# Three of four batches written out by channels, in a convolution-attention kernel on one core

## The chip, the cores and the metric

The kernel runs on one core of one Trainium2 chip. A core has five engines, which run side by side and wait for one another by semaphores: TensorE (PE in the profile, PEld for its weight loads), VectorE (DVE), ScalarE (ACT), GpSimd (POOL) and SyncE (SP). In this kernel nearly all DMAs are issued by SP, one after another in the order of its queue. The metric is device time in microseconds, the median of several runs.

## The reference

The input `x` has 4 batches of 128 channels by 64 x 64 positions; the 4096 positions are the tokens. All is float32.

```
# layer 0, per batch
q, k, v = wq @ x, wk @ x, wv @ x                 # 64 channels each
x  = x + wo @ (softmax(k^T q, axis=2) v)         # 4096 x 4096 scores
# layer 1, on tokens t = x^T
t  = t + softmax(causal(LN(t) Wq (LN(t) Wk)^T / sqrt(128))) LN(t) Wv
w  = batchnorm(LN(t) W)                          # mean and variance over batches and tokens
y_0 = 0;  y_n = sigmoid(w_n + y_(n-1) V^T)       # a recurrence over the 4096 tokens
out = (t + y)^T
```

## The kernel before, in words

The function `fast_path` does all the work; a second, general path stands behind a branch on `flag` and is not entered here.

**Attention.** Batches go one after another, and in each batch layer 0 and then layer 1, in eight blocks of 512 tokens. A list `items` holds pairs of key tiles; a loop over it interleaves on TensorE the scores of one item with the values of the item two before. Everything else (projections, normalization, transposes) is cut into steps that generators hand out at due slots (`push`, `waiting`, `side`). The result of a block stays in the tile `xs`, by tokens. In `finish1`, the end of a block of layer 1, `third` replaces that block in `xs` by `w`, the input of the recurrence. The sum `t`, which the output still needs, is saved to DRAM before that, in one of two forms. For the batches below `BY_C`, the step `kept` transposes it in squares of 32 x 32 on VectorE and writes it by channels to `x2c` with four DMAs. For the others, one DMA stores it by tokens to `x2t` (in `first`).

**Start.** SP issues eight loads of `x` for batch 0 (L426), then the transfers `swap` of the keys (L541) and the loads of `x` by tokens (`tokens0`, L585), in an order that the scheduler chose.

**Recurrence.** It is computed for 256 chunks of 16 tokens at once (`STEPS` 16, `NCH` 256). Ten steps of a warm-up (`WARM`) give each chunk a start value, then 16 steps follow. In each step and for each of the four batches there is a product with V on TensorE (L1153), an add of `w` on VectorE (L1155, tile `z`) and a sigmoid on ScalarE (L1158). The last block's end in `third` is written out apart (`final`): two half projections (L825), two copies into `xs` (L827), and the function `warm`, which issues products that nobody reads. A test compares the last states with the start values (`gap`, `count`, `total`) and sets `flag`.

**Output.** For the batches by channels, `xc` is loaded from `x2c`, four loads for each batch (L1093). After every step, `add` sums state and `xc` for those batches on GpSimd (L1165, tile `sum`, three buffers) and one DMA writes the step out (L1167). The adds and these DMAs are kept in program order. For the batches by tokens, `xr` is loaded from `x2t` (L1103); `residual` transposes the states on TensorE (L1182), adds them to `xr` on VectorE (L1184) and writes pieces of 512 KB (L1187). The `residual` of the last batch stands at the program's end, behind the test.

```
for s in range(-WARM, STEPS):
    for b in range(B):
        step(b, s)
    if s >= 0:
        add(s)
```

Of the kernel before, what the change touches and what calls it, by code (L numbers as in the profile page):

```python
# [9 lines left out]
F32 = mybir.dt.float32  # L10
AF = mybir.ActivationFunctionType
ALU = mybir.AluOpType
AX = mybir.AxisListType
PSUM = bass.MemoryType.PSUM

P = 128
BLK = 512
# [1 line left out]
LN_EPS = 1e-5  # L19
BN_EPS = 1e-5  # L20
STEPS = 16
BY_C = 2


@with_exitstack
def general_path(
# [259 lines left out]
    with tc.tile_pool(name="wx", bufs=1) as wxp, tc.tile_pool(name="fwork", bufs=3) as wk:  # L286
# [28 lines left out]
        with tc.tile_pool(name="ys", bufs=3) as ysp, tc.tile_pool(  # L315
# [13 lines left out]
            for kb in range(nblk):  # L329
# [15 lines left out]
                K = STEPS // S  # L345
                for b in range(BY_C):
                    oc = ysp.tile([P, S, K], F32, tag="oc", name="oc")
                    nc.vector.tensor_copy(oc, o[:, b].rearrange("p (k s) -> p s k", s=S))
                    nc.sync.dma_start(out=out_c[b, :, :, ts(kb, K)], in_=oc)
                op = ps_o.tile([P, B - BY_C, P], F32, tag="o", name="oT_ps")  # L350
                for b in range(BY_C, B):
                    nc.tensor.transpose(op[:, b - BY_C, :], o[:, b, :], ident)
                oT = ysp.tile([P, B - BY_C, P], F32, tag="oT", name="oT")
                nc.vector.tensor_copy(oT, op)
# [5 lines left out]
def fast_path(  # L360
# [22 lines left out]
    nc = tc.nc  # L383
    B, C, N = x.shape
    M = c_wqT.shape[1]
    assert C == P and M == P // 2 and N % CHUNK == 0
    NT = N // P
    NB = N // BLK
    TPB = BLK // P
    SHIFT = 32.0  # L390
    LOW, HIGH = 1e-25, 1e25
    WARM, TOL = 10, 2e-6
# [12 lines left out]
    xs = xpool.tile([P, B, N], F32, name="xs")  # L405


    x2c = dram.tile([BY_C, NB, S, Q, BLK], F32, name="x2c")
    x2t = dram.tile([B - BY_C, N, P], F32, name="x2t")
# [18 lines left out]
    ident = const.tile([P, P], F32, name="ident")  # L428
    make_identity(nc, ident)
    ones = const.tile([P, 1], F32, name="ones")  # L430
# [30 lines left out]
    good = const.tile([P, 2], F32, name="good")  # L461
# [20 lines left out]
    with tc.tile_pool(name="batch", bufs=1) as batch, tc.tile_pool(name="rows", bufs=2) as rowp, tc.tile_pool(  # L482
        name="prob", bufs=4
    ) as prob, tc.tile_pool(name="work", bufs=2) as wk, tc.tile_pool(name="stat", bufs=4) as stat, tc.tile_pool(
        name="ps_s", bufs=2, space=PSUM
    ) as ps_s, tc.tile_pool(name="ps_a", bufs=1, space=PSUM) as ps_a, tc.tile_pool(
        name="ps_m", bufs=2, space=PSUM
    ) as ps_m:

        def misc(name):  # L490
            return ps_m.tile([P, BLK], F32, tag="m", name=name)
# [90 lines left out]

        def tokens0(b, g):

            nc.sync.dma_start(  # L585
                out=xs[:, b, ts(g, BLK)].rearrange("p (j c) -> p j c", c=P),
                in_=xT[b, ts(g, BLK)].rearrange("(j p) c -> p j c", p=P),
            )

        def rows1(b, g):  # L590
            ps = misc("r_ps")
            nc.tensor.matmul(ps, lhsT=g1, rhs=bs[b].xhT[:, ts(g, BLK)], start=True, stop=True)
            r = rowp.tile([P, BLK], F32, tag="r", name="rows1")
            nc.scalar.copy(r, ps)
            bs[b].next.append(r)
# [100 lines left out]
        def in_range(last):  # L696

            r = recs.rearrange("p l b t -> p (l b t)")
            r = r[:, -TPB:] if last else r[:, :-TPB]
            r2 = wk.tile([P, BLK], F32, tag="den", name="r2")[:, : r.shape[-1]]  # L700
            nc.vector.tensor_scalar(r2, r, LOW, None, ALU.is_ge)
            nc.vector.tensor_scalar(r, r, HIGH, None, ALU.is_le)
            nc.vector.tensor_tensor(r, r, r2, ALU.mult)
            nc.vector.tensor_reduce(good[:, 1:2] if last else good[:, 0:1], r, AX.X, ALU.add)
# [50 lines left out]
        def finish1(b, g):  # L755
            agg, den = bs[b].agg, bs[b].den
            mem = {}
            final = b == B - 1 and g == NB - 1

            def warm(n, rhs):  # L760

                ps = ps_s.tile([P, 2 * BLK], F32, tag="s", name="warm_ps")
                for _ in range(n):
                    tc.keep_in_program_order(
                        nc.tensor.matmul(ps[:, : BLK // 2], lhsT=ident, rhs=rhs, start=True, stop=True)
                    )
# [51 lines left out]
            def third():  # L818

                to = xs[:, b, ts(g, BLK)].rearrange("p (s c) -> p s c", s=STEPS)  # L820
                if final:
                    in_range(True)
                    for k in range(2):
                        wp = misc("wx_ps")[:, : BLK // 2]
                        nc.tensor.matmul(wp, lhsT=wfc, rhs=mem["xhT"][:, ts(k, BLK // 2)], start=True, stop=True)  # L825
                        nc.vector.bn_stats(ends[:, 3 + 6 * k : 9 + 6 * k], wp)
                        nc.scalar.copy(to[:, :, ts(k, CPB // 2)], wp.rearrange("p (c s) -> p s c", s=STEPS))  # L827
                    warm(6, xs[:, b, ds(g * BLK, BLK // 2)])
                    return
                wp = misc("wx_ps")  # L830
                nc.tensor.matmul(wp, lhsT=wf, rhs=mem["xhT"], start=True, stop=True)
                nc.vector.bn_stats(stats[:, b * NB + g], wp)  # L832
                if b == B - 1 and g == NB - 2:
                    ahead()
                    in_range(False)
                nc.scalar.copy(  # L836
                    to.rearrange("p s (j q u) -> p s j q u", q=Q, j=TPB),
                    wp.rearrange("p (q j u s) -> p s j q u", q=Q, j=TPB, s=STEPS),
                )
# [244 lines left out]
    with tc.tile_pool(name="xr", bufs=1) as xrp, tc.tile_pool(name="y", bufs=2) as yp, tc.tile_pool(  # L1084
        name="sums", bufs=3
    ) as sums, tc.tile_pool(
        name="ps_y", bufs=1, space=PSUM
    ) as ps_y, tc.tile_pool(name="ps_r", bufs=4, space=PSUM) as ps_r:

        xc = xrp.tile([P, BY_C, NCH, STEPS], F32, name="xc")  # L1090
        for b in range(BY_C):
            for c in range(Q):
                nc.sync.dma_start(  # L1093
                    out=xc[ts(c, S), b].rearrange("r (g k) s -> r g (k s)", g=NB),
                    in_=x2c[b, :, :, c].rearrange("g r n -> r g n"),
# [3 lines left out]
        by_chunk = lambda t: t.rearrange("b (h q s) c -> b h q s c", q=P, s=STEPS)  # L1099
        xr = xrp.tile([P, B - BY_C, HALVES, STEPS, P], F32, name="xr")  # L1100
# [19 lines left out]
        by_step = xs.rearrange("p b (g s c) -> p b s g c", s=STEPS, c=CPB)  # L1120
        start = xrp.tile([P, B, NCH + 1], F32, name="start")
        nc.gpsimd.memset(start[:, :, 0:1], 0.0)
        prev = [None] * B
        grid = lambda t: t.rearrange("p (g c) -> p g c", c=CPB)
        pair = lambda t: t.rearrange("p (h q) -> p h q", q=P)
# [8 lines left out]
        def states(b, s):  # L1134
            if b < BY_C:
                return by_step[:, b, s]
            return pair(early[:, b - BY_C, s]) if s < TPB else late[:, b, s // TPB - 1, s % TPB]
# [20 lines left out]
                nc.scalar.activation(y, shaped(z), AF.Sigmoid, bias=shift)  # L1158
            prev[b] = start[:, b, :NCH] if s == -1 else y

        def add(s):

            t = sums.tile([P, BY_C, NCH], F32, tag="sum", name="sum")
            by_grid = lambda t: t.rearrange("p b (g c) -> p b g c", c=CPB)
            ins = nc.gpsimd.tensor_tensor(by_grid(t), by_step[:, :BY_C, s], by_grid(xc[:, :, :, s]), ALU.add)  # L1165
            tc.keep_in_program_order(ins)
            tc.keep_in_program_order(nc.sync.dma_start(out=out_c[:, :, s].rearrange("b c k -> c b k"), in_=t))  # L1167

        for s in range(-WARM, STEPS):
            for b in range(B):  # L1170
                step(b, s)
            if s >= 0:
                add(s)

        def residual(b):

            for h in range(HALVES):
                for s0 in range(0, STEPS, TPB):
                    part = slice(s0 - TPB, s0 + TPB)
                    ps = ps_r.tile([P, TPB, P], F32, tag="r", name="yT_ps")  # L1180
                    for j in range(TPB):
                        nc.tensor.transpose(ps[:, j], states(b, s0 + j)[:, h], ident)  # L1182
                    t = xr[:, b - BY_C, h, ds(s0, TPB)]
                    nc.vector.tensor_tensor(t, t, ps, ALU.add)  # L1184
                    if s0 % (2 * TPB):
                        tc.keep_in_program_order(
                            nc.sync.dma_start(out=by_chunk(out_t)[b - BY_C, h, :, part], in_=xr[:, b - BY_C, h, part])  # L1187
                        )

        for b in range(BY_C, B - 1):  # L1190
            residual(b)


        gap = xrp.tile([P, B], F32, name="gap")
        for b in range(B):
            ps = ps_y.tile([P, NCH], F32, tag=f"y{b}", name="gap_ps")
            nc.tensor.matmul((grid if b < BY_C else pair)(ps), lhsT=ident, rhs=prev[b], start=True, stop=False)
            nc.tensor.matmul(ps, lhsT=minus, rhs=start[:, b, 1:], start=False, stop=True)
            sq = yp.tile([P, NCH], F32, tag=f"y{b}", name="sq")
            nc.scalar.activation(sq, ps, AF.Square, accum_out=gap[:, b : b + 1])  # L1200
        count = xrp.tile([P, B + 2], F32, name="count")
        nc.vector.tensor_scalar(count[:, :B], gap, TOL * TOL, None, ALU.is_le)
        nc.vector.tensor_copy(count[:, B:], good)
        total = xrp.tile([P, 1], F32, name="total")
        nc.vector.tensor_reduce(total, count, AX.X, ALU.add)
        tp = ps_y.tile([1, 1], F32, tag="y0", name="tp")
        nc.tensor.matmul(tp, lhsT=total, rhs=ones, start=True, stop=True)
        nc.vector.tensor_scalar(flag, tp, P * (B + 2 * B * NT) - 0.5, None, ALU.is_lt)
        residual(B - 1)


# [62 lines left out]
```

## Time and profile before

| | |
|---|---|
| runs | 2058.35, 2058.4 and 2059.66 us; median 2058.4 us |
| profiled execution | 2059.29 us, of which the profile's span is 2057.6 us |
| mean granted TensorE clock | 0.997 |
| busy over the span | TensorE 99%, VectorE 72%, ScalarE 48%, GpSimd 7% |
| attention | from the start to 1974.3 us, the copy of the last values |
| recurrence | the first product of a step at 1991.94, the last sigmoid until 2039.5 us |
| GpSimd's adds | 16 of 1.54 us, from 2010.9 us on |
| `xc` loads | 8 of 512 KB, issued from 1974.3 to 1981.4 us |
| `xr` loads | 4 of 1024 KB, issued from 1981.9 to 1988.7 us |

Times in the profile count from the start of the span. A timeline line gives the start, the length, the engine, the source line, the operation, output and inputs, and in brackets how long the engine had been idle before and what ended that. A line of a tile's view gives the shortest, median and longest duration in nanoseconds and the first and last start. A line of stretches gives the stretch, its length, the busy time of TensorE, its weight loads, VectorE, ScalarE and GpSimd with their counts, the granted clock, the share of the DMA engines and GB/s.

### The profile page before, as it was taken

The page shows a single profiled execution, that of the slowest core. Times are in us where ns is not written, and L with a number is a line of the kernel's source. Part 1 is how long each engine was busy: PE and PEld are TensorE (multiplying, and loading weights), DVE is VectorE, ACT ScalarE, POOL GpSimd, SP SyncE. Part 2 cuts the span into 40 slices and gives each one's busy share as a digit, 9 for nine tenths or more (in the row PEclk, how much of TensorE's full clock was granted, in tenths as well). Part 3 has the DMA queues.
Part 4 walks back from the last instruction along what each step waited for, and adds up shares of the span by engine and source line. Part 5 has one row for each costly group of instructions (what it writes and reads, how often), then busy time and mean ns, then how long its engine had stood idle before and what let it go on. Part 6 is the DMA issues. An engine that isn't in the chain of part 4 may idle for free. (4 is left out here: it accounts for less than half of the span.)

```text
span 2057.6 us, 30790 instructions
## 1 busy us (share of the span) xinstructions
PE 2039.1 (99%) x11646; PEld 909.0 (44%) x11646; DVE 1486.6 (72%) x2862; ACT 988.8 (48%) x1071; POOL 137.5 (7%) x237
## 2 busy tenths in 40 slices
PE   9999999999999999999999999999999999999998
PEld 3643355444333345444433335444433334544456
DVE  4899877554889987555689987654488998765568
ACT  5666633333666653333466663233366665333346
POOL 1000011000000011000000001100000000100004
PEclk9999999999999999999999999999999999999999
DMA  4111021231201112223111101123000111111064
GB/s 113 43 23 23 12 42 37 55 76 36 58 5 20 22 22 42 47 63 71 27 43 22 22 12 42 42 67 77 16 17 2 23 22 22 47 36 32 16 161 174
DMA packets 237293, 89.03 MB, mean 43 GB/s; under 512 B 174688, under 2 KB 219232, under 8 KB 236624
## 3 DMA queue, kind: packets, MB, share of 16 engines
q1 hardware_dynamic: 236128, 86.42, 17.7%
q8 instruction: 93, 1.52, 0.3%
q14 instruction: 64, 0.52, 0.1%
q0 software_dynamic: 288, 0.39, 0.1%
q10 hardware_dynamic: 720, 0.16, 0.0%
HBM read 45.84 MB, written 36.89 MB: 40 GB/s over the span
## 5 line engine op out<-in xcount | busy, mean ns | idle before, releaser
L931 DVE TENSOR_TENSOR dsum<-dsum,p 128x1024 f32<-128x1024 f32 x676 | 826.3, 1222 | 428.7 <-ACT p L907 308.1
L905 ACT ACTIVATE p<-s_ps,nshift 128x1024 f32<-128x1024 f32 x512 | 569.3, 1116 | 317.7 <-PE s_ps L891 311.4
L907 ACT ACTIVATE p<-s_ps 128x1024 f32<-128x1024 f32 (+2 forms) x288 | 274.2, 952 | 609.4 <-PE s_ps L900 607.1
L951 PE MATMUL acc<-p,v 64*64 64x512 f32 x4096 | 543.0, 590 | 0.0
L891 PE MATMUL s_ps<-swap,kr 64*64 64x512 f32 x2048 | 538.9, 591 | 1.4 <-ACT p L905 0.9
L891 PE MATMUL s_ps<-kr 64*64 64x512 f32 x2048 | 524.9, 591 | 0.0
L900 PE MATMUL s_ps<-rows,xhT 128*128 128x512 f32 (+3 forms) x1152 | 502.9, 559 | 0.0
L959 PE MATMUL acc<-p,xh 128*128 128x512 f32 (+3 forms) x1152 | 500.8, 557 | 0.0
L959 PEld LDWEIGHTS acc<-p,xh 128*128 128x128 f32 x1152 | 216.2, 190 | 244.3 <-issue 234.2
L900 PEld LDWEIGHTS s_ps<-rows,xhT 128*128 128x128 f32 x1152 | 214.0, 190 | 243.3 <-issue 203.2
L951 PEld LDWEIGHTS acc<-p,v 64*64 64x64 f32 x4096 | 166.6, 133 | 272.5 <-issue 251.6
L891 PEld LDWEIGHTS s_ps<-swap,kr 64*64 64x64 f32 x2048 | 151.4, 133 | 131.6 <-issue 107.8
L891 PEld LDWEIGHTS s_ps<-kr 64*64 64x64 f32 x2048 | 140.7, 133 | 138.0 <-issue 133.8
L663 POOL TENSOR_TENSOR ln_rstd<-ln_var,mhalf 128x4 f32<-128x4 f32 x64 | 68.1, 1065 | 1099.5 <-DVE ln_var L661 1099.5
L939 DVE TENSOR_TENSOR dsum<-dsum,p 128x256 f32<-128x256 f32 (+1 forms) x120 | 55.4, 498 | 64.6 <-POOL p L911 64.6
L649 DVE SCALAR_TENSOR_TENSOR xs<-o_ps,recs,xs 128x128 f32<-128x128 f32 x256 | 74.5, 341 | 3.1
L679 DVE TENSOR_SCALAR xh<-xs,ln_mv,ln_rstd 128x128 f32<-128x128 f32 x252 | 70.3, 343 | 2.2
L911 POOL TENSOR_SCALAR_AFFINE_SELECT p<-p 128x128 f32<-128x128 f32 x128 | 35.9, 304 | 486.2 <-ACT p L907 473.8
L658 DVE BATCH_NORM_STATS2 ln_st<-xs 128x6 f32<-128x128 f32 x256 | 63.3, 270 | 0.0
L929 DVE COPY dsum<-p 128x1024 f32<-128x1024 f32 x60 | 41.0, 683 | 15.4 <-ACT p L907 10.8
L1155 DVE SCALAR_TENSOR_TENSOR z<-xs,scale,y_ps 128x256 f32<-128x256 f32 x100 | 44.6, 481 | 9.1 <-PE y_ps L1153 7.7
L836 ACT COPY xs<-wx_ps 128x512 f32<-128x512 f32 x31 | 18.1, 585 | 65.6 <-DVE stats L832 61.5
(148 smaller groups left out, 993.7 us busy)
## 6 DMA issues: line engine op xcount, KB each, us to landing
xs<-in_xT SPq DMA_DIRECT2D x32, 256.0 KB, 3.0
by_r<-sqT SPq DMA_DIRECT2D x128, 64.0 KB, 2.2
xhT<-by_r SPq DMA_DIRECT2D x128, 64.0 KB, 2.0
by_c<-sqT SPq DMA_DIRECT2D x124, 64.0 KB, 1.8
xhT<-by_c SPq DMA_DIRECT2D x31, 256.0 KB, 2.7
xs<-in_x SPq DMA_DIRECT2D x12, 512.0 KB, 5.6
swap<-kr SPq DMA_DIRECT2D x32, 128.0 KB, 2.3
x2c<-sqT SPq DMA_DIRECT2D x64, 64.0 KB, 2.3
```

The costliest lines, as they stand in the source:

```text
L649: nc.vector.scalar_tensor_tensor(t, in0=op[:, ts(j, P)], scalar=rec[:, j : j + 1], in1=t, op0=ALU.mult, op1=ALU.add)
L658: nc.vector.bn_stats(st[:, j], xs[:, b, ds(g * BLK + j * P, P)])
L663: nc.gpsimd.tensor_tensor(y, var, mhalf, ALU.pow)
L679: nc.vector.tensor_scalar(dst[:, j], xs[:, b, ds(g * BLK + j * P, P)], mv[:, j, 0:1], y[:, j : j + 1], ALU.subtract, ALU.mult)
L891: nc.tensor.matmul(ps[c * M : c * M + M, off : off + n], lhsT=bs[it.b].kr[part, h, ds(t % (NT // 2) * P + c * M, M)], rhs=rows[h], start=True,
L900: nc.tensor.matmul(ps[:, off : off + n], lhsT=lhsT, rhs=rhs, start=True, stop=True)
L905: nc.scalar.activation(it.p[:, :off], ps[:, :off], AF.Exp, bias=nshift)
L907: nc.scalar.activation(it.p[:, :off], ps[:, :off], AF.Exp, scale=float(P) ** -0.5)
L931: nc.vector.tensor_tensor(flat, flat, it.p, ALU.add)
L939: nc.vector.tensor_tensor(den[:, h, q0:], den[:, h, q0:], it.p[:, o : o + n], ALU.add)
L951: nc.tensor.matmul(bt.acc[h * M : h * M + M, r], lhsT=bt.v[part, t % (NT // 2), t // (NT // 2)], rhs=it.p[part, o : o + n], start=it.first ...
L959: nc.tensor.matmul(bt.acc[:, 0, q0:], lhsT=bt.xh[:, t], rhs=it.p[:, o : o + n], start=it.first and h == 0, stop=it.last and h == 1,)
```

## The change

Batch 2 joins the batches by channels (`BY_C` 3): `x2c` and `xc` hold three batches, `x2t` and `xr` one. GpSimd sums the steps 0 to 13, 768 columns instead of 512 at a time; VectorE sums steps 14 and 15 at the end. The `residual` of the last batch moves ahead of the test, and its second half is written in four pieces of 256 KB. The unread products in `third` read `xhT` instead of the block of `xs` that the copies write; in the built program the two copies now stand ahead of the first sigmoid on ScalarE. The loads by tokens of batch 0 are kept in program order, and in the built program three of them stand behind all eight `swap` transfers on SP, the others further back.

```
-BY_C = 2
+BY_C = 3
...
-            nc.sync.dma_start(
+            dma = nc.sync.dma_start(
                 out=xs[:, b, ts(g, BLK)].rearrange("p (j c) -> p j c", c=P),
...
+            if b == 0:
+                tc.keep_in_program_order(dma)
...
-                    warm(6, xs[:, b, ds(g * BLK, BLK // 2)])
+                    warm(6, mem["xhT"][:, : BLK // 2])
...
+        BY_POOL = STEPS - 2
-        def add(s):
+        def add(s, engine=nc.gpsimd):
...
-            if s >= 0:
+            if 0 <= s < BY_POOL:
                 add(s)
...
-                    nc.vector.tensor_tensor(t, t, ps, ALU.add)
-                    if s0 % (2 * TPB):
-                        tc.keep_in_program_order(
-                            nc.sync.dma_start(out=by_chunk(out_t)[b - BY_C, h, :, part], in_=xr[:, b - BY_C, h, part])
-                        )
+                    tc.keep_in_program_order(nc.vector.tensor_tensor(t, t, ps, ALU.add))
+                    if pairs and h == 0 and not s0 % (2 * TPB):
+                        continue
+                    part = slice(s0 - TPB, s0 + TPB) if pairs and h == 0 else slice(s0, s0 + TPB)
+                    tc.keep_in_program_order(
+                        nc.sync.dma_start(out=by_chunk(out_t)[b - BY_C, h, :, part], in_=xr[:, b - BY_C, h, part])
+                    )
...
+        residual(B - 1)
         for b in range(B):
...
-            nc.tensor.matmul((grid if b < BY_C else pair)(ps), lhsT=ident, rhs=prev[b], start=True, stop=False)
+            tc.keep_in_program_order(nc.tensor.matmul((grid if b < BY_C else pair)(ps), lhsT=ident, rhs=prev[b], start=True, stop=False))
...
+        for s in range(BY_POOL, STEPS):
+            add(s, nc.vector)
+        got.append(judge())
+        nc.vector.tensor_scalar(flag, got[0], P * (B + 2 * B * NT) - 0.5, None, ALU.is_lt)
-        residual(B - 1)
```

The function `judge` holds the instructions of the test that stood there before (`count`, `total`, the product `tp`), pinned to program order.

More of the change, by code (lines that the diff above doesn't have):

```diff
@@ L1159, in step @@
             prev[b] = start[:, b, :NCH] if s == -1 else y
-        def add(s):
+        BY_POOL = STEPS - 2
+        def add(s, engine=nc.gpsimd):
             t = sums.tile([P, BY_C, NCH], F32, tag="sum", name="sum")
             by_grid = lambda t: t.rearrange("p b (g c) -> p b g c", c=CPB)
-            ins = nc.gpsimd.tensor_tensor(by_grid(t), by_step[:, :BY_C, s], by_grid(xc[:, :, :, s]), ALU.add)
+            ins = engine.tensor_tensor(by_grid(t), by_step[:, :BY_C, s], by_grid(xc[:, :, :, s]), ALU.add)
             tc.keep_in_program_order(ins)
@@ L1171, in fast_path, with residual @@
                 step(b, s)
-            if s >= 0:
+            if 0 <= s < BY_POOL:
                 add(s)
-        def residual(b):
+        def residual(b, pairs=True, then=None):
             for h in range(HALVES):
                 for s0 in range(0, STEPS, TPB):
-                    part = slice(s0 - TPB, s0 + TPB)
                     ps = ps_r.tile([P, TPB, P], F32, tag="r", name="yT_ps")
@@ L1183, in residual @@
                     t = xr[:, b - BY_C, h, ds(s0, TPB)]
-                    nc.vector.tensor_tensor(t, t, ps, ALU.add)
-                    if s0 % (2 * TPB):
-                        tc.keep_in_program_order(
-                            nc.sync.dma_start(out=by_chunk(out_t)[b - BY_C, h, :, part], in_=xr[:, b - BY_C, h, part])
-                        )
+                    tc.keep_in_program_order(nc.vector.tensor_tensor(t, t, ps, ALU.add))
[5 more added lines that the diff above has]
+                    )
+                if then and h == 0:
+                    then()
         for b in range(BY_C, B - 1):
@@ L1194, in fast_path, with judge @@
         gap = xrp.tile([P, B], F32, name="gap")
+        count = xrp.tile([P, B + 2], F32, name="count")
+        nc.vector.tensor_copy(count[:, B:], good)
+        def judge():
+            total = xrp.tile([P, 1], F32, name="total")
+            tc.keep_in_program_order(nc.vector.tensor_scalar(count[:, :B], gap, TOL * TOL, None, ALU.is_le))
+            tc.keep_in_program_order(nc.vector.tensor_reduce(total, count, AX.X, ALU.add))
+            tp = ps_y.tile([1, 1], F32, tag="y0", name="tp")
+            nc.tensor.matmul(tp, lhsT=total, rhs=ones, start=True, stop=True)
+            return tp
+        got = []
+        residual(B - 1)
         for b in range(B):
             ps = ps_y.tile([P, NCH], F32, tag=f"y{b}", name="gap_ps")
-            nc.tensor.matmul((grid if b < BY_C else pair)(ps), lhsT=ident, rhs=prev[b], start=True, stop=False)
+            tc.keep_in_program_order(nc.tensor.matmul((grid if b < BY_C else pair)(ps), lhsT=ident, rhs=prev[b], start=True, stop=False))
             nc.tensor.matmul(ps, lhsT=minus, rhs=start[:, b, 1:], start=False, stop=True)
@@ L1200, in fast_path @@
             nc.scalar.activation(sq, ps, AF.Square, accum_out=gap[:, b : b + 1])
[L1201 to L1208, printed above, removed]
-        residual(B - 1)
+        for s in range(BY_POOL, STEPS):
+            add(s, nc.vector)
+        got.append(judge())
+        nc.vector.tensor_scalar(flag, got[0], P * (B + 2 * B * NT) - 0.5, None, ALU.is_lt)
 def kernel(
```

## The prediction

> **What bounds the kernel now.** The page comes first. TensorE is busy for the whole span, so up to the last attention product only an idle TensorE costs time; the chain of waits holds nothing but the last add, so the end has to be rebuilt from the timeline.
>
> ```profile
> PE 2039.1 (99%) x11646; PEld 909.0 (44%) x11646; DVE 1486.6 (72%) x2862; ACT 988.8 (48%) x1071; POOL 137.5 (7%) x237
> DVE xr L1184 0%
> ```
>
> Second, the timeline of TensorE and ScalarE between the last attention product and the recurrence, and the one-microsecond stretches around it (the third number from the end is the granted clock).
>
> ```profile
> 1985.22 0.60 ACT L1150 ACTIVATE y<-xs,shift_half,scale 128x256 f32<-128x256 f32 x1 [3.61 <-DVE shift L1118]
> 1985.72 0.62 ACT L827 COPY xs<-wx_ps 128x256 f32<-128x256 f32 x2
> 1986.40 5.49 PE L765 MATMUL warm_ps<-xs,ident 128*128 128x256 f32 x12 [3.78 <-ACT xs L827]
> 1991.94 2.53 PE L1153 MATMUL y_ps<-y,vf 128*128 128x256 f32 x9
> ...
> 1985.00:1986.00 1.00, 0.00 (x0) 0.00 (x0) 0.19 (x2) 0.78 (x3) 0.00 (x0) 0.76 1.07 199
> 1991.00:1992.00 1.00, 0.94 (x4) 0.22 (x2) 0.00 (x0) 0.00 (x0) 0.00 (x0) 0.50 1.05 203
> 1993.00:1994.00 1.00, 1.00 (x7) 0.65 (x5) 1.00 (x3) 0.57 (x2) 0.00 (x0) 1.00 1.06 207
> ```
>
> The six unread products read the block that ScalarE writes at L827, so they start at 1986.40, after 3.78 us without a matmul. By then the granted clock is 0.50; they take 5.49 us, and the first product of the recurrence waits behind them although its operand was ready near 1985.8.
>
> Third, the tile views of `xc` and `sum`, and the queue of SP at the end.
>
> ```profile
> L1093 SPq DMA_DIRECT2D xc<-x2c x8: 303/486/932, 1974.3 to 1981.4; - x8
> DMA to landing us min/median/max: 4.6/11.1/17.4
> ...
> L1165 POOL TENSOR_TENSOR sum<-xs,xc x16: 1531/1536/1551, 2010.9 to 2038.8; 128x512 f32<-128x512 f32 x16
> DMA to landing us min/median/max: 2.1/2.1/2.9
> ...
> 2012.41 28.29 SPq L1167 DMA_DIRECT2D out_x<-sum  x16
> 2040.80 9.89 SPq L1187 DMA_DIRECT2D out_x<-xr  x8
> ```
>
> GpSimd's add (1.54 us) fits into a step of the recurrence (1.815 us: TensorE's weight loads begin at 2003.07, 2004.88, 2006.70). The eight `xc` loads land one after another: the second, issued at 1977.5, lands 6.1 us later at 1983.6, the eighth at 1981.4 + 17.4 = 1998.8, so 2.53 us each. After the recurrence, 4 MB of `xr` go out; the last, issued at 2050.35, lands 4.8 us later at 2055.1, and the program's end adds 2.5 us: 2057.6.
>
> Fourth, the period of a batch, by the copy that ends the second convolution block, and TensorE's stall at a batch's start.
>
> ```profile
> 573.80 1.00 ACT L973 COPY half<-acc 128x1024 f32<-128x1024 f32 x1
> 1065.31 1.00 ACT L973 COPY half<-acc 128x1024 f32<-128x1024 f32 x1
> 1555.87 1.00 ACT L973 COPY half<-acc 128x1024 f32<-128x1024 f32 x1
> 1037.20 0.65 PE L891 MATMUL s_ps<-swap,kr 64*64 64x512 f32 x2 [0.46 <-ACT p L905]
> ```
>
> Batch 1, which is kept by channels, takes 491.51 us, batch 2 by tokens 490.56; the 0.46 us stall stands at the starts of batches 1 and 2, not of 3.
>
> **The change, part by part, on the clock of the profile before.**
>
> *Batch 2 by channels, in the attention.* Eight `kept` steps (a VectorE transpose of 0.68 us and four DMAs each) replace eight `x2t` stores. In the changed program batch 2's order on TensorE, VectorE and ScalarE is the same as batch 1's, so its price is the difference of the periods: +0.95 us. Below nothing it cannot well go, as batch 0's period (82.28 to 573.80) is 491.5 too.
>
> *Loads by tokens behind the keys' transfers.* At the start TensorE loses 0.53 us at 12.81 to the first `swap` transfer, issued at 8.7 and landed 4.1 us later. It already stands ahead of every load by tokens; behind the 2 MB of `x` it stays. I take 0; the bound is a gain of 0.5. The loads pass all eight transfers and now leave after 32.8 instead of 9.8; their first reader is the join after the third block (109.75), so 70 us cover them, and the denominators' DMAs queued behind come at 55.
>
> *The unread products.* With `xhT` they follow the last projection at 1982.6. Six at full clock cost 2.7 us (the nine at L765 before them took 4.05), ending at 1985.3. The copies of L827 now precede the first sigmoid, in a slot in which ScalarE idles 3.6 us; that sigmoid, bound by `shift`, still runs from 1985.2 to 1985.8. So the first product starts near 1985.9, its `z` near 1986.5 instead of 1992.92, and the recurrence ends 6.4 us earlier. TensorE's gap is 0.6 us; the clock fell only after 3.1 us (1982.6 to about 1985.75). [...]
>
> *What is late next: GpSimd.* Step 0 of batch 2 would be ready at 2011.2 − 6.4 = 2004.8. But the first add needs all `xc` loads, now twelve: 1998.8 + 4 × 2.53 = 2008.9. So 4.1 of the 6.4 us are lost here. The two `xr` loads queued behind land by 2014; VectorE reads them only near 2032.
>
> An add of 128x768 is not in the trace. Purely in proportion it costs 1.5 × 1.536 = 2.30 us. GpSimd's small adds-by-power show a fixed part: 128x1 (L1111) 0.547, 128x4 (L663) 1.065, hence 0.37 at zero columns; with that, 0.37 + 1.5 × (1.536 − 0.37) = 2.12. Taking all of 0.547 as fixed gives 2.03. I take 2.12, as both anchor rows are tensor-tensor instructions of this engine. Fourteen, back to back: 29.7 us (28.4 to 32.2), ending at 2038.6. Each output's buffer is free two adds later (4.2 us, against a landing of 2.5), so no wait is added there.
>
> [...]
>
> *VectorE's tail.* The last `z` ends at 2038.9 − 6.4 = 2032.5; eight adds of `xr` at 0.605 end at 2037.4; two sums of 768 columns at some 0.95 (between 0.687 for 512 and 1.222 for 1024) would end at 2039.3. The second waits for the buffer of GpSimd's thirteenth add (2036.5 + 2.6 = 2039.1) and ends at 2040.1. The test now stands behind it: `flag` near 2043, still ahead of the last landing.
>
> *The last outputs.* SP issues in order: all `xr` pieces, ready since 2037.4, wait for GpSimd's fourteenth sum at 2038.6. From there: that sum lands after 2.1 + 0.4 = 2.5 us (384 instead of 256 KB), two pieces of 512 KB at 1.30 (as in 2042 to 2047, near 400 GB/s), four of 256 KB at 0.69, two sums at 1.17: 2038.65 + 2.5 + 2.6 + 2.8 + 2.3 = 2048.9. Before, the same count came out 2.2 us short: 2042.5 + 8 × 1.30 = 2052.9 against 2055.1, partly because the test held SP up between 2043.8 and 2046.7. I add 1.5 (0 to 2.2): 2050.4. Nine issues at 0.37 us do not bind.
>
> **Sum.** 2050.4 + 2.5 = 2052.9, plus 0.95 for batch 2: a span of 2053.8, 3.8 us less. The profiled execution, 2059.3 us for that span, would become 2055.5; from the median of 2058.4 it is 2054.6. A measurement of this kernel can tell 0.2% (4.1 us) from no change, so this lies just inside "the same".
>
> **Rivals.** *Faster:* GpSimd's add is at its lower bound (−1.3) and the last packets go out without stragglers (−1.5), with perhaps some of the 0.5 at the start: 2051.3 to 2053.3. For it: the fixed part; against: the copies of `xc` have a stride of 16 elements, which may cost per element. *The clock closes anyway:* if the gap is longer than I read, the recurrence keeps its place, batch 2's first state comes at 2011.2 rather than the load at 2008.9, and the time is 2.3 us more, 2056.9. Against it: a gap of 0.6 us. *Slower:* the add grows faster than its columns, since VectorE works beside it all the time. It decides the sign from 2.12 + 3.8/14 = 2.39 us, and is slower by over 0.2% from 2.69; at 2.9 us the time is 2054.6 + 14 × 0.78 = 2065.5. Against it: all sixteen adds took 1.531 to 1.551 us beside a VectorE busy for 97%. *No effect of the loads by tokens* is already in the sum.
>
> **Chances.** My sum within its bounds 0.60; faster 0.27; the clock 0.08; slower 0.05. Of the first, about 0.18 falls below 2054.3, the line of 0.2%, so faster gets 0.45, the same 0.50, slower 0.05. The range goes from 2052.0, where add and stragglers are both low, to 2057.7, where add (+2.5) and stragglers (+0.7) are both high.
>
> **What would show it.** Right: unread products at 1982.6 and no clock of 0.50 before the end; first add of GpSimd near 2009.9 (0.95 later than on the old clock), held by `xc`, adds of about 2.1 us without idle time between; `xr` outputs issued right behind the fourteenth sum; a period of 491.5 us for batch 2. Wrong: a first add before 2006 (the loads are faster than I think), adds above 2.4 us, or a recurrence that still begins near 1992.

## The result, and the profile after

The changed kernel takes 2057.11 us (median of 12 runs, 2056.48 to 2058.35), the kernel before, run beside it, 2059.1 us (12 runs, 2058.22 to 2060.6). The ratio is 0.9989, 95% interval [0.9981, 0.9997]: about 2 us less, which is inside the 0.2% that the prediction called no change. The profiled execution took 2056.48 us with a span of 2054.8 us, 2.8 us less than the 2057.6 of before; the sum had said 3.8.

The page, its first part: TensorE is still busy all the time.

```profile
PE 2033.6 (99%) x11614; PEld 904.7 (44%) x11614; DVE 1489.1 (72%) x2864; ACT 989.3 (48%) x1071; POOL 143.2 (7%) x235
```

The timeline between the attention and the recurrence:

```profile
1983.26 2.75 PE L768 MATMUL warm_ps<-xhT,ident 128*128 128x256 f32 x12
1983.54 0.76 ACT L830 COPY xs<-wx_ps 128x256 f32<-128x256 f32 x2 [1.12 <-DVE ends L829]
1986.18 2.08 ACT L1153 ACTIVATE y<-xs,shift_half,scale 128x256 f32<-128x256 f32 x4 [1.88 <-DMA xc<-x2c]
1986.83 6.46 PE L1156 MATMUL y_ps<-y,vf 128*128 128x256 f32 x27 [0.82 <-ACT y L1153]
```

And the first of the one-microsecond stretches that showed the clock at 0.50 before (the third number from the end is the granted clock):

```profile
1991.00:1992.00 1.00, 1.00 (x7) 0.64 (x5) 1.00 (x3) 1.00 (x3) 0.00 (x0) 1.00 1.07 201
```

The unread products follow the last projection without a gap and take 2.75 us instead of 5.49; TensorE then waits 0.82 us for the sigmoid, and the granted clock stays at 1.00 where it was 0.50. The recurrence starts at 1986.83 instead of 1991.94.

The view of the tile `xc`, and the timeline of the end:

```profile
L1170 POOL TENSOR_TENSOR sum<-xs,xc x14: 2182/2196/2231, 2010.4 to 2038.6; 128x768 f32<-128x768 f32 x14
L1096 SPq DMA_DIRECT2D xc<-x2c x12: 303/532/1126, 1975.2 to 1989.7; - x12
L1170 DVE TENSOR_TENSOR sum<-xs,xc x2: 1444/2166/2887, 2039.2 to 2042.0; 128x768 f32<-128x768 f32 x2
...
DMA to landing us min/median/max: 4.7/15.1/20.7
```

```profile
2010.44 30.38 POOL L1170 TENSOR_TENSOR sum<-xs,xc 128x768 f32<-128x768 f32 x14 [25.47 <-PE y_ps L1156]
...
2033.60 4.86 DVE L1188 TENSOR_TENSOR xr<-xr,yT_ps 128x512 f32<-128x512 f32 x8
...
2039.24 4.25 DVE L1170 TENSOR_TENSOR sum<-xs,xc 128x768 f32<-128x768 f32 x2 [0.78 <-ACT sq L1221]
...
2041.31 5.02 SPq L1193 DMA_DIRECT2D out_x<-xr  x6
...
2044.13 0.15 DVE L1225 TENSOR_SCALAR flag<-tp 1x1 int32<-1x1 f32 x1 [0.37 <-PE tp L1211]
2046.43 1.77 SPq L1172 DMA_DIRECT2D out_x<-sum  x2
```

Here the gain is lost again. The last of the twelve `xc` loads is issued at 1989.7 and lands 20.4 us later, at 2010.05. GpSimd begins 0.39 us after that. The releaser in brackets is a product, which was done long before the load; it is the load that came last. GpSimd then adds for 30.38 us without a pause and ends at 2040.82. VectorE's adds of `xr` are done at 2038.46, but their outputs are queued on SP behind GpSimd's fourteenth sum and leave from 2041.31 on. The last output lands at 2052.71, and the program ends 2.1 us later.

The period of batch 2, by the same copy as before, and the stall at the start of batch 3:

```profile
1065.19 1.00 ACT L976 COPY half<-acc 128x1024 f32<-128x1024 f32 x1
...
1528.57 0.65 PE L894 MATMUL s_ps<-swap,kr 64*64 64x512 f32 x2 [0.44 <-ACT p L908]
...
1556.68 1.00 ACT L976 COPY half<-acc 128x1024 f32<-128x1024 f32 x1
```

It is now 491.49 us, where it was 490.56: +0.93. The stall that stood at the starts of batches 1 and 2 stands at that of batch 3 too.

### The profile page after: what moved, and what is told of

Read it like the earlier page. It is cut to its first block, busy times and chain, and to the rows that moved or that the text cites. A ratio compares the mean times of both kernels' runs of the same rounds, so it can differ in the third digit from the quotient of the medians.

```text
span 2054.8 us, 30765 instructions
## 1 busy us (share of the span) xinstructions
PE 2033.6 (99%) x11614; PEld 904.7 (44%) x11614; DVE 1489.1 (72%) x2864; ACT 989.3 (48%) x1071; POOL 143.2 (7%) x235
## 4 chain that ended last, share of the span: by engine, by line
PE 98%; DVE 1%; ACT 0%; issue 0%; DMA 0%; POOL 0%; ACTq 0%; POOLq 0%; DVEq 0%
PE s_ps L903 22%; PE acc L962 22%; PE s_ps L894 22%; PE acc L954 21%; PE o_ps L642 3%; PE y_ps L1156 2%; PE r_ps L595 1%; PE wx_ps L834 1%; PE kr_ps L535 1%; PE v_ps L547 1%; ACT p L908 0%; PE warm_ps L496 0%; DMA swap<-kr 0%; DVE sum L1170 0%; PE yT_ps L1186 0%
```

## The experiments

Twelve kernels, each beside the kernel before. Since an execution's start varies (the first `half` copy begins between 54.72 and 55.92 us), the table also gives the part after the attention: the span less the start of the last `agg` copy. From the first `half` copy to that last `agg` copy it is 1919.5 us in each kernel with two batches by channels and 1920.4 in each with three, so the 0.93 us of batch 2 is there every time.

| kernel | median us | ratio to before [95%] | span | after the attention |
|---|---|---|---|---|
| before | 2058.6 to 2059.1 | 1 | 2057.6 | 83.3 |
| changed | 2057.11 | 0.9989 [0.9981, 0.9997] | 2054.8 | 79.7 |
| e1_warm_only | 2053.98 | 0.9977 [0.9967, 0.9987] | 2052.2 | 77.3 |
| e5_warm_tokens | 2053.92 | 0.9975 [0.9965, 0.9985] | 2052.2 | 77.3 |
| e2_old_warm | 2058.35 | 0.9995 [0.9986, 1.0004] | 2056.8 | 81.3 |
| e3_pool12 | 2057.26 | 0.9994 [0.9985, 1.0003] | 2055.4 | 80.2 |
| e4_xr_first | 2057.68 | 0.9995 [0.9986, 1.0004] | 2055.2 | 79.6 |
| e8_three_better | 2055.08 | 0.9982 [0.9973, 0.9991] | 2052.9 | 77.7 |
| e6_contiguous | 2053.3 (1 run) | | 2051.6 | 75.8 |
| e7_wide_loads | 2053.32 | 0.9972 [0.9961, 0.9983] | 2051.2 | 75.9 |
| e9_two_better | 2054.18 | 0.9977 [0.9968, 0.9986] | 2052.8 | 77.8 |
| e10_wide_right | 2092.36 | 1.0161 [1.0147, 1.0175] | 2090.9 | 115.3 |
| e11_wide_order | 2053.29 | 0.9972 [0.9962, 0.9982] | 2052.0 | 75.9 |
| e12_all | 2053.0 | 0.9970 [0.9960, 0.9981] | 2052.0 | 75.7 |

### The parts alone

**e1_warm_only**, the kernel before with one line changed:

```
-                    warm(6, xs[:, b, ds(g * BLK, BLK // 2)])
+                    warm(6, mem["xhT"][:, : BLK // 2])
```

> The kernel before, with only the operand of the six unread products changed. Theory (the earlier recurrence is worth its whole 6 us as long as nothing behind it is late: with two batches by channels the eight xc loads land by 1998.8 and the four xr loads by 2009.4, both before they are read): first product of the recurrence near 1986.0, first add of GpSimd near 2004.7 held by the state and not by a load, span 2051.2 to 2051.8, time ratio to before about 0.997. Rival (what the full change gained, 2.8 us of span, is all that the earlier recurrence can bring, because the outputs' transfers set the end anyway): span near 2054.8, ratio 0.9987.

```profile
2005.42 1.54 POOL L1165 TENSOR_TENSOR sum<-xs,xc 128x512 f32<-128x512 f32 x1 [20.64 <-DMA xr<-x2t]
2035.36 9.89 SPq L1187 DMA_DIRECT2D out_x<-xr  x8
```

GpSimd starts 5 us earlier than in the changed kernel (it needs eight loads, not twelve), stays within the recurrence's step, and the outputs of `xr` leave from 2035.36. The bracket names a load of `xr` that landed just then. But in e5 and e9 the add starts as long after the first product of the recurrence (18.8 us), although that load landed 0.25 and 0.43 us before the add; so it is the state that holds it. One line alone takes 4.8 us off the kernel before: more than the whole change.

**e2_old_warm**, the changed kernel with that line undone.

> The changed kernel, with only the operand of the unread products put back. Theory (the first add waits for the twelfth xc load, so most of the earlier recurrence is unused): first product of the recurrence near 1992.8, first add near 2012.1 instead of 2010.4, held by the state of batch 2, and a span 1.7 us longer than the changed kernel's, 2056.5. Rival (the recurrence sets the end, the loads do not matter): 5.9 us longer, 2060.7.

```profile
1987.50 5.07 PE L768 MATMUL warm_ps<-xs,ident 128*128 128x256 f32 x12 [3.78 <-ACT xs L830]
2011.78 30.43 POOL L1170 TENSOR_TENSOR sum<-xs,xc 128x768 f32<-128x768 f32 x14 [26.52 <-ACT xs L1161]
```

The slow products are back and the recurrence starts 5.8 us later (1992.62), yet the span is only 2.0 us longer, 1.7 of it after the attention, and the median 1.2 us: GpSimd's first add moves by 1.3 us, from the load (2010.44) to the state (2011.78). So in the changed kernel the line is worth 1 to 2 us, not 6, because the load holds GpSimd back. The other parts without the line can't be told from nothing: 0.9995, with an interval up to 1.0004.

**e5_warm_tokens**, e1 with the loads by tokens kept in program order.

> The kernel before with two parts of the change: the other operand of the unread products, and the loads by tokens of batch 0 in program order. It is to be compared with the kernel that has the operand alone (2053.98 us). Theory (the first swap transfer stands ahead of these loads in either order, so they are worth nothing that can be told): within 0.4 us of it. Rival (the loads take bandwidth from the first swap transfer): 0.5 us or more less, and TensorE's wait before the first scores is gone.

The same time as e1. TensorE's wait for the first transfer of the keys was 0.53 to 1.03 us in the three profiles with the old order of the loads and 0 to 1.44 us in the eleven with the new one (0.58 in e5): it varies by execution, and the order is worth nothing that can be measured.

### Moving work at the end

**e3_pool12** gives VectorE four sums instead of two.

```
-        BY_POOL = STEPS - 2
+        BY_POOL = STEPS - 4
```

> The changed kernel with 12 steps on GpSimd and 4 on VectorE. Theory (GpSimd's chain of adds holds the outputs queued behind it): the xr outputs leave SP right after the twelfth sum, near 2036.6 instead of 2041.3, the last output lands 2 to 4 us earlier, and the span falls by 1 to 3 us to 2051.8 to 2053.8; it is limited by the test, which stands behind four sums on VectorE (near 2045, instead of 2044.1). Rival (GpSimd's chain is covered, the volume of the outputs sets the end): within 0.5 us of 2054.8, or later by the two VectorE sums, 2.9 us.

**e4_xr_first** issues the sums of steps 12 and 13 behind the outputs of `xr`.

```
-            if 0 <= s < BY_POOL:
+            if 0 <= s < BY_POOL - 2:
...
+        for s in range(BY_POOL - 2, BY_POOL):
+            add(s)
```

> The changed kernel with the six xr outputs moved ahead of the sums of steps 12 and 13 on SP; the adds stay where they are. Theory (the queue's order, not the transfer volume, puts the xr outputs behind GpSimd): the xr outputs leave from 2035 to 2039, the last sum lands near 2046.5 instead of 2052.7; what then ends last is the branch after the test (flag at 2044.1, TensorE's branch until 2050.8), so the span is about 2052.9, 1.9 us less. Rival (the transfers are limited by their volume and not by when they are queued): last landing near 2052, span within 0.5 us of 2054.8.

VectorE's last sum in the timeline of e3; then, of e4, the same sum, the test's last instruction and the tile view of VectorE's two sums:

```profile
2046.47 1.46 DVE L1170 TENSOR_TENSOR sum<-xs,xc 128x768 f32<-128x768 f32 x1 [3.77 <-DMA out_x<-sum]
```

```profile
2046.25 1.46 DVE L1170 TENSOR_TENSOR sum<-xs,xc 128x768 f32<-128x768 f32 x1 [3.67 <-DMA out_x<-sum]
2048.36 0.15 DVE L1227 TENSOR_SCALAR flag<-tp 1x1 int32<-1x1 f32 x1 [0.37 <-PE tp L1211]
...
L1170 DVE TENSOR_TENSOR sum<-xs,xc x2: 1458/2116/2773, 2039.8 to 2046.3; 128x768 f32<-128x768 f32 x2
```

In both, the outputs of `xr` leave some 3.7 us earlier (2037.68 and 2037.47 instead of 2041.31), and nothing is gained: VectorE's last sum then waits 3.7 us for a buffer, whose output is now queued behind those of `xr`, and the test behind it sets `flag` 4.5 and 4.2 us later than in the changed kernel. I had not expected that wait. The outputs themselves did come earlier: the last one lands at 2050.49 and 2050.26, not at 2052.71. But the program now ends 6.8 us after `flag` is set, in both, and 4.9 us after the last landing. So the span of e4 is the rival's, and its reason is not: the queue's order did hold the outputs back, and the late test took the gain.

**e8_three_better** takes that wait away: e4 with six buffers for the sums, and the test ahead of VectorE's sums.

> The changed kernel with the xr outputs ahead of the sums of steps 12 and 13, six buffers for the sums instead of three, and the test ahead of VectorE's two sums. Theory (in the two runs with earlier xr outputs the gain was lost to VectorE's last sum, which waited 3.7 us for a buffer whose transfer stood behind the xr outputs, and with it the test): no wait for a buffer, flag near 2041.5, last landing near 2047.3, span 2049.3 to 2051, ratio to before 0.996 to 0.997. Rival (the end is bound by the volume of outputs): span 2054 or more.

```profile
2042.08 2.81 DVE L1170 TENSOR_TENSOR sum<-xs,xc 128x768 f32<-128x768 f32 x2 [0.16 <-DMA out_x<-xr]
2042.44 4.06 SPq L1172 DMA_DIRECT2D out_x<-sum  x4
```

The wait is gone and 1.9 us of span are gained on the changed kernel (2.0 in the median, though the intervals of the two ratios overlap), half of the least that I expected. The result lies between theory and rival. The four last sums, issued from 2042.44 on, land only 5.8 to 6.0 us after their issue; the last piece of `xr`, issued before them, lands at 2044.96. A stretch of e8 says what limits them:

```profile
2041.00:2049.00 8.00, 0.19 (x2) 0.11 (x2) 3.29 (x5) 0.01 (x1) 0.14 (x1) 0.68 1.01 348
```

Through these eight microseconds the DMA engines are busy all the time (a mean share of 1.01, 348 GB/s): here the volume of the outputs is the limit, as the rival has it, and another order within this stretch could not bring much.

### What holds GpSimd

**e6_contiguous**: the sums read neighbouring elements of `xc` instead of every sixteenth. These are not the elements that belong to the step, so this kernel shows a price and not a remedy.

```
-by_step[:, :BY_C, s], by_grid(xc[:, :, :, s]), ALU.add)
+by_step[:, :BY_C, s], by_grid(xc.rearrange("p b k s -> p b (k s)")[:, :, ts(s, NCH)]), ALU.add)
```

> The changed kernel, in which the sums read xc without its stride of 16 elements (256 neighbouring elements of the same tile, so other values are added; nothing else differs). First theory (the stride is what made VectorE's sum 1.44 us alone instead of the 0.95 expected, and part of GpSimd's 2.20): VectorE's near 0.95 alone, GpSimd's at 2.0 or less. Rival (the stride costs nothing): 1.44 and 2.20 as before, so it is the 96-byte to 128-byte pieces of the other operand or the engines' shared access.

```profile
L1170 POOL TENSOR_TENSOR sum<-xs,xc x14: 1818/1833/1848, 2011.9 to 2035.2; 128x768 f32<-128x768 f32 x14
L1170 DVE TENSOR_TENSOR sum<-xs,xc x2: 951/952/953, 2039.0 to 2039.9; 128x768 f32<-128x768 f32 x2
```

The stride costs GpSimd 0.36 us (2.196 against 1.833) and VectorE 0.49 us (1.444 against 0.952). Without it GpSimd's adds start 1.77 us apart, within a step of the recurrence (1.815 us), where they took 2.17 with it, and the span of this one run is 3.2 us shorter.

**e7_wide_loads**: each `xc` load spans all 128 partitions and a quarter of the tokens, instead of 32 partitions and all tokens. The channels land in other rows, so the sums are not those of the reference; the work is the same.

```
-            for c in range(Q):
+            for h in range(4):
...
-                    out=xc[ts(c, S), b].rearrange("r (g k) s -> r g (k s)", g=NB),
-                    in_=x2c[b, :, :, c].rearrange("g r n -> r g n"),
+                    out=xc[:, b].rearrange("p (g k) s -> p g (k s)", g=NB)[:, ts(h, NB // 4)],
+                    in_=x2c[b].rearrange("g r c n -> (r c) g n")[:, ts(h, NB // 4)],
```

> The changed kernel, with each xc load spread over 128 partitions instead of 32 (same bytes, same packets of 2 KB, same number of loads; the channels land in another order, so the by-channel outputs get other rows added). Theory (the last xc landing sets GpSimd's first add, and GpSimd's chain the last outputs): the loads land at 1.3 us each instead of 2.6, all by 1997; the first add starts at 2005.5 to 2006 when batch 2's state is there; the chain ends near 2036; the span falls to 2052.0 to 2052.5, where the branch after the test becomes the limit. Rival (the loads are limited by their 2 KB packets, not by the 32 partitions): landings as before, first add at 2010.4, span 2054.8.

Five microseconds of the loads in the changed kernel, and then in e7 (the last two numbers are the share of the DMA engines' time that was busy, and GB/s):

```profile
1990.00:1995.00 5.00, 5.00 (x24) 3.28 (x22) 4.95 (x12) 5.00 (x12) 0.00 (x0) 1.00 1.06 205
```

```profile
1987.00:1992.00 5.00, 4.98 (x22) 3.35 (x22) 4.20 (x10) 5.00 (x11) 0.00 (x0) 1.00 1.05 394
```

GpSimd in the timeline of e7:

```profile
2006.22 30.44 POOL L1170 TENSOR_TENSOR sum<-xs,xc 128x768 f32<-128x768 f32 x14 [21.07 <-ACT xs L1161]
```

With 32 partitions the engines are as busy (1.06 against 1.05) and move half as much (205 against 394 GB/s). The wide loads land 1.36 us apart instead of 2.55, the last at 1996.25; GpSimd is now held by the state and starts 4.2 us earlier. Its chain of adds is as long as before (30.44 against 30.38 us), so this run shows the gate by itself: 3.6 us of span, 3.8 in the median.

**e10_wide_right** puts every channel in its own place: one load per block of 512 tokens, gathered from four groups of rows.

```
+            for g in range(NB):
...
+                    out=xc[:, b].rearrange("p (g k) s -> p g (k s)", g=NB)[:, g],
+                    in_=x2c[b, g].rearrange("r c n -> c r n"),
```

> The changed kernel with xc loaded over all 128 partitions at a time, with every channel in its own place: 24 loads of 256 KB, one for each block of 512 tokens, instead of 12 of 512 KB over 32 partitions. First theory (the loads' pitch is a matter of the 32 partitions): the loads land at 0.65 to 0.8 us each, the last before 2000; GpSimd's first add is held by the state, near 2006, and the span is 2051.2 +- 0.5, as in the run with the wide loads. Rival (a load that is wide but smaller, or gathers its partitions from four places, loses the gain): the last load lands after 2004, and the span is 2052.5 or more.

A stretch of five microseconds, and GpSimd in the timeline:

```profile
1990.00:1995.00 5.00, 3.05 (x7) 2.52 (x8) 1.05 (x3) 3.54 (x8) 0.00 (x0) 0.53 0.26 101
```

```profile
2047.03 30.05 POOL L1170 TENSOR_TENSOR sum<-xs,xc 128x768 f32<-128x768 f32 x14 [61.57 <-DMA xc<-x2c]
```

A miss on the far side of the rival: 34 us slower than before. In this stretch a quarter of the DMA engines' time is used, at 101 GB/s. The recurrence too starts 5 us later than in the changed kernel, at 1991.95, because, by the profile, the copies into `xs` waited for the store of `x2t`, which reads that block. The source's slowest dimension has four entries here, and 32 or 128 in the other kernels; whether the share of 0.26 comes from that, no run shows.

**e11_wide_order** gets the same places by another order of `x2c` in DRAM, with rows of 512 bytes, and a tile `sq` ordered to match. **e12_all** is e11 with e8's order of the outputs, six buffers and the earlier test.

```
-    x2c = dram.tile([BY_C, NB, S, Q, BLK], F32, name="x2c")
+    x2c = dram.tile([BY_C, NB, TPB, Q, S, P], F32, name="x2c")
...
+                    out=xc[:, b].rearrange("p (g k) s -> p g (k s)", g=NB * TPB)[:, ts(h, NB)],
+                    in_=x2c[b].rearrange("g j c r n -> (c r) (g j) n")[:, ts(h, NB)],
```

> The changed kernel with xc loaded over all 128 partitions, every channel in its own place, by another order of x2c in DRAM (rows of 512 bytes instead of 2 KB): 12 loads of 512 KB as in the changed kernel, and the same number of writes. First theory (the pitch comes from the 32 partitions of a load): the loads land 1.3 to 1.9 us apart, the last before 2003; the first add is held by the state near 2006, and the span is 2051.2 +- 0.5, as in the run with the wide loads. Rival (rows of 512 bytes cost as much as the 32 partitions did): a pitch of 2.2 us or more, the first add after 2007.5, and a span of 2052.5 or more.

> The kernel of e11_wide_order with the outputs of xr ahead of the sums of steps 12 and 13, six buffers for the sums, and the test ahead of VectorE's two sums. First theory (the order of the outputs still costs): the outputs of xr leave as their adds end, from about 2035.5, and the last landing is 1.0 to 1.5 us earlier than in e11_wide_order, span 2049.5 to 2050.3. Rival (the bytes that are left after the recurrence and the program's end set the time): the same span within 0.4 us.

```profile
2007.07 30.41 POOL L1171 TENSOR_TENSOR sum<-xs,xc 128x768 f32<-128x768 f32 x14 [21.06 <-ACT xs L1162]
```

In e11 the loads land 1.8 us apart, the last at 2001.21; the state holds GpSimd, and the time is that of e7. (Its span is 0.8 us longer than e7's because this execution started 0.85 us later; the part after the attention is the same.) In e12 the outputs of `xr` leave 1.9 us earlier than in e11, and the span is the same, the median 0.3 us less. That is the rival's number, but its reason is not shown: with the test ahead of them VectorE's sums start at 2043.09 instead of 2039.43, so the last sum is issued 2.1 us later (2045.93 against 2043.79), and between 2043 and 2048 the DMA engines have some time to spare (shares of 0.87 and 0.80). The early outputs gave and the late sums took; the order of the outputs alone was not run on e11.

**e9_two_better**: e1 with the first half of the last `residual` ahead of the test.

```
+        residual(B - 1, [0])
...
-        residual(B - 1)
+        residual(B - 1, [1])
```

> The kernel before with the new operand of the unread products, and the first half of the last batch's residual ahead of the test, so that VectorE does not wait for the test's last states. First theory (VectorE's last adds set the end): VectorE's last add ends near 2044.1 instead of 2044.9, the last landing follows about 4.4 us later instead of 4.8, span 2050.9 +- 0.4, ratio to the kernel before 0.997. Rival (the 4 MB of the last outputs set the end, whenever VectorE is done): span 2052.2 +- 0.4, as with the operand alone.

The fifth and sixth piece leave 1.6 us earlier than in e1, but the last two now wait for the test (issued at 2044.06 and 2045.26, 0.3 us later than in e1) and land 5 us after that. The first theory falls: VectorE was not done earlier (2045.2), and the time is e1's within its interval.

Of the versions that write every sum in its place, e8 (2055.1), e1, e5 and e9 with two batches by channels (2053.9 to 2054.2), and e11 and e12 with three (2053.3 and 2053.0) lie below both kernels. Against the kernel before this is clear in all of them. Against the changed kernel it is less so: only the interval of e12 stays clear of its interval, those of e1, e5, e9 and e11 overlap it by 0.06% or less, and that of e8 by 0.1%. Of all, e12 is the lowest, but its interval and that of e1 overlap.

## Why the prediction was right or wrong

The time lies in the range, 2.5 us above the forecast, and it is "the same", the likeliest case. Of the 2.5 us, 1.0 is error of the sum (a profiled execution of 2056.48 instead of 2055.5); the rest is that the profiled execution of before lay 0.9 above its median, and that of after 0.6 below.

| step | predicted (on the new clock) | measured |
|---|---|---|
| batch 2 by channels | +0.95 | +0.93 |
| loads by tokens | 0 | 0 (e5 against e1) |
| first product | 1986.85 | 1986.83 |
| last `xc` landing | 2009.85 | 2010.05 |
| GpSimd's first add | 2009.85 | 2010.44 |
| one add | 2.12 | 2.17 from one to the next |
| GpSimd done | 2039.55 | 2040.82 |
| a sum on VectorE | 0.95 | 2.89 and 1.44 |
| fourteenth sum's issue to the last landing | 11.75 | 11.86 |
| end of the program | 2.5 | 2.1 |

- The sum's error is GpSimd: 0.6 us of a later start and 0.7 us of pace, with 0.1 in the outputs and 0.4 less at the program's end.
- **The add of 768 columns** was the term that mattered most, and its fixed part was too large. The 0.37 came from two small instructions that raise to a power, at 0.17 us for each column more; the adds themselves, 1.536 for 512 columns and 2.196 for 768, leave 0.22 fixed, and 0.22 + 1.5 × (1.536 − 0.22) is 2.19 instead of 2.12. The stride, named only under the rivals as what "may cost per element", is no error of this sum, since the add of 512 columns has it too; but it costs 0.36 of the 2.196. Without it the add takes 1.833, below the lower bound of 2.03.
- **VectorE's sums** were interpolated from instructions with neighbouring elements; 0.95 is what they take without the stride (e6). The step was wrong by 0.5 for the second, and by 1.9 for the first, which lay beside GpSimd's last add. It cost nothing here, since SP was behind GpSimd anyway.
- **"Nine issues at 0.37 us do not bind"** was wrong in its figure: the two pieces of 512 KB and four of 256 KB took SP 5.02 us, the last two sums 1.77. The time from the first issue to the last landing still came out (11.86 against 11.75), with some luck: it holds 1.5 us that were added for stragglers without a mechanism. In the trace the landings stand still for 2.6 us (2047.69 to 2050.33), and from 2047.10 on two queues of instructions, which move nothing between 2035 and 2047, move nine packets of 8 and 16 KB. Whether these hold the outputs up was not tested.
- **The buffer** of VectorE's second sum was seen as a wait of 1 us that costs little. With the outputs in another order it became 3.7 us and, through the test, ate the whole gain of e3 and e4.
- **The gate of `xc`** was the right mechanism at the right size: 4.1 of 6.4 us were forecast as lost there. What I did not draw from it is that the line on the unread products alone, with eight loads and adds of 1.54 us, would be faster than the whole change: 2053.98 against 2057.11. On top of that line, the rest of the change costs 3.1 us by the medians; wide loads (e7) or adds without the stride (e6) each win that much back.
- **The clock** stayed at 1.00 until 2043.66, as forecast, but the reading behind it was off. In the profile of before it fell at 1985.52, 2.9 us after the last product and not 3.1; and in e2, with the same gap of 3.78 us, 1.5 us after it (at 1985.18, the product ending at 1983.72). One row was not enough to call a gap short enough; 0.82 us happens to lie below both. The third number from the end in these stretches, of before and of e2, is the clock:

```profile
1985.50:1985.60 0.10, 0.00 (x0) 0.00 (x0) 0.00 (x0) 0.10 (x1) 0.00 (x0) 0.59 0.87 164
```

```profile
1985.10:1985.20 0.10, 0.00 (x0) 0.00 (x0) 0.00 (x0) 0.00 (x0) 0.10 (x1) 0.93 1.19 225
```

- The range's ends are 0.2 and 0.1 us inside what their terms add up to (2051.8 and 2057.8).
- The rivals: the clock did not close, as e2 shows by its contrast. No add of 768 columns on GpSimd took more than 2.28 us in any of the runs, so the slower case, from 2.39 on, did not come. The faster case needed an add below 2.12 us, and only e6, without the stride, has it.

## What to carry to other kernels

When an early stage is shortened, first find what will be late next, and price the change's own additions against that new limit: here four more loads and half again as much work for GpSimd (2.20 instead of 1.54 us an add) went exactly where the freed time was. Test the parts one by one; one line did better than the bundle it came in. And moving an output forward in a queue moves another one back, with its buffer and whatever waits for that buffer.

## What the runs showed of the hardware

- **A stride of 16 elements (64 bytes)** in one operand of two: in the changed kernel 768 columns on GpSimd take 2.196 instead of the 1.833 us of e6 (+20%), on VectorE 1.444 instead of 0.952 (+52%).
- **VectorE and GpSimd, both with two operands in SBUF:** in the changed kernel VectorE's first sum starts at 2039.24 and takes 2.89 us; GpSimd's last add ends at 2040.82, 1.31 us before that sum's end. In e4 it starts at 2039.81, takes 2.77 us, and ends 1.30 us after GpSimd; in e10 it takes 2.65 us and again ends 1.30 us after GpSimd. Alone it takes 1.44. So in these three cases it seems to wait for GpSimd's instruction to end; why, no run shows.
- **Loads onto 32 partitions** move 205 GB/s at a DMA share of 1.06 in the changed kernel, those onto 128 move 394 at 1.05 in e7, 1.9 times as much.
- **SP's issue** of a piece of 256 KB takes 0.60 to 1.17 us in the changed kernel, where four follow one another, against 0.33 us for the pieces of 512 KB in e1.
- **The granted clock** fell from 1.00 to 0.50 at no fixed time after TensorE's last product: 2.9 us after it in the kernel before, 1.5 us in e2, 3.8 us in e10 (1990.33 after 1986.50).
